# A four-layer graph network on one core: quarter-transposed projections, pre-added row sums, and a scheduler that weighs age against remaining path

One core of one Trainium2 chip (trn2), float32 throughout. The metric is device time of one execution in microseconds (us), lower is better. Engine names: PE is TensorE, PEld its weight loads, DVE is VectorE, ACT is ScalarE, POOL is GpSimd, SP is SyncE (here it only issues DMAs; "SPq" is its queue). A "graph" below is one of the 32 batch elements.

## The reference

`x` is (32, 512, 256), `adj` a (512, 512) 0/1 matrix with about 6% of ones. Each of the four layers is a residual and a normalisation around an attention over the graph:

```
x = LN(x + transformer_block(x, adj))   # 8 heads of 32, FFN; gains are 1, biases 0 in the inputs
x = LN(x + gat(x, adj))                 # layer 1: softmax_m(leaky_relu(s1[n] + s2[m])) @ (x W)
x = LN(x + bilinear_gat(x, adj))        # layer 2: softmax(leaky_relu(x W1 W2^T x^T)) @ (x W3), relu
x = LN(x + gat4(x, adj))                # layer 3: as layer 1 with 4 heads, elu
```

## The kernel before

The kernel is one straight instruction stream per engine. A small planner in Python, run when the kernel is built, decides everything: each operation carries a cost for each engine that may do it, and the planner simulates the engines with these costs, picks the next operation, its engine and its buffers, and emits it. Each engine then executes its instructions in that order; an instruction that waits holds all behind it on that engine. The costs are written in by hand.

```python
# Plan.run: choosing the next operation                        (cut)
tmin = min(c[0] for c in cands)
s, o, e = min((c for c in cands if c[0] <= tmin + 0.05),
              key=lambda c: (not c[1].frees, c[1].graph, -c[1].rank))   # oldest graph first
...
plan = Plan(slots, {...buffer reserves...}, 4, {"DVE": 0.5})            # four graphs open

F = 0.86                                # planner's costs, us: 512 columns on PE
TR = 0.113                              # one PE transpose
TT = {"DVE": cdve(1024)}                # 1024-column tensor_tensor on VectorE
TP = {"POOL": 2.35}                     # 1024-column tensor_tensor on GpSimd

def transposed(xs):                     # 8 PE transposes and 2 evacuations
    ...
            for k in range(KC):
                for j in range(2):
                    nc.tensor.transpose(two(ps)[:, k, j*P:(j+1)*P], T4(xs)[:, 2*s+j, k*P:(k+1)*P], ident)
        op({"PE": 4 * TR}, fn, r=[xs[s]], w=[ps], pre=[xT])
        evac(ps, xT, s, nodes(s), two)

# normalisation, per half of a graph: statistics on DVE, four two-column GpSimd operations, apply on ACT or DVE
op({"DVE": 0.92}, stats, ...)           # bn_stats, bn_aggr
op({"POOL": 1.6}, scales, ...)          # add, pow, negate, multiply
op({"DVE": 0.325, "ACT": cact(C, 2)}, norm, ...)
# checks of value ranges: one to three tiny GpSimd operations
op({"POOL": 0.17 * (1 if lo is None else 3)}, fn, r=[t], ...)

# layer 0: row sums, "packed" is four heads side by side on PE  (cut)
def sums(e, g=g, p=p, ps_s=ps_s):
    for m in (0, 2):
        packed(ps_s, p, m, lambda h: pick[:, g, :], m == 0, m == 2)
op({"PE": 2 * F + 0.13}, sums, r=[p[0][0], p[1][0], p[0][2], p[1][2]], w=[ps_s], pre=[sT])
# layer 0: two wide operations on GpSimd, 128x1024, both inputs in SBUF
op(TP, lambda e: tt(e, T4(xs), T4(xs), be2_sb.t.unsqueeze(1)..., ALU.add), r=[xs, be2_sb], w=[xs])
op(TP, lambda e: tt(e, T4(u), T4(u), g1_sb.t.unsqueeze(1)..., ALU.mult), r=[u, g1_sb], w=[u])

# layers 1 and 3: projection with the score columns
for c in range(NC):
    for i in range(KC):
        nc.tensor.matmul(ps.t[:, :C+e3], T2(xT)[:, i, c*P:(c+1)*P], w.t[:, i, :], start=(i==0), stop=(i==KC-1))

# a graph's start: x in blocks of 32x32, by eight DMAs of 64 KB from the SP queue
op({"SP": 0.8}, block, w=[xZ])
```

## Time and profile before

| | before |
|---|---|
| median of 4 executions | 3234.03 us (3230.48 to 3234.76) |
| profiled span | 3232.5 us |
| PE work, each record at its start-to-start price | 2832 us |
| span less PE work | 400 us |
| PE work / time, 160 to 2960 us ("middle efficiency") | 0.903 |

"Work" is used all through: every PE record is counted at the price that the prediction derives (for instance 0.430 us for a 512-column record), so that the modelled, overlapping ends of matmuls don't blur the sum. The middle efficiency is that work divided by the 2800 us of the window.

### The profile page before, as it was taken

Reading aid. Unit: us, or ns where it says so; the run is one execution under the profiler, and the core shown is the slowest. Engines: PE = TensorE matmul, PEld = TensorE weight load, DVE = VectorE, ACT = ScalarE, POOL = GpSimd, SP = SyncE. Lnnn points to the kernel's source line nnn. Section 1 sums busy time; section 2 is a strip of 40 time slices with the busy share of each in tenths; the row PEclk is TensorE's granted clock in tenths of the full one; section 3 lists DMA queues with packets and bytes.
Section 4 is the critical chain, followed back from the end, with each engine's and each line's share of the span. In section 5 each row is a group of like instructions: output and inputs, shape, how many; then the busy total and the mean of one; then the engine's idle time right before and its main releaser. Section 6 shows DMA issues by size and latency. Waiting matters only on the chain. (4 is left out here: it accounts for less than half of the span.)

```text
span 3232.5 us, 47121 instructions
## 1 busy us (share of the span) xinstructions
PE 3070.4 (95%) x16827; PEld 1892.0 (59%) x16858; DVE 2472.0 (76%) x4819; ACT 1673.5 (52%) x3425; POOL 1278.0 (40%) x2418
## 2 busy tenths in 40 slices
PE   6999999999999999999999999999999999999976
PEld 3656665565656656646656646656646666646543
DVE  6777679777788787797787797777797777797763
ACT  3554555545654555554555554555554555454532
POOL 0434345243444333354233454333354334364330
PEclk8999999999999999999999999999999999999987
DMA  5010110011101110101110111010111010110000
GB/s 123 4 37 14 40 34 24 17 37 34 37 24 37 37 34 21 34 24 37 36 34 20 34 24 37 28 43 10 44 24 37 25 45 4 50 24 24 24 24 21
DMA packets 200338, 101.43 MB, mean 31 GB/s; under 512 B 151585, under 2 KB 186913, under 8 KB 200097
## 3 DMA queue, kind: packets, MB, share of 16 engines
q1 hardware_dynamic: 200096, 98.35, 11.5%
q8 instruction: 135, 2.21, 0.3%
q14 instruction: 107, 0.87, 0.1%
HBM read 81.20 MB, written 17.10 MB: 30 GB/s over the span
## 5 line engine op out<-in xcount | busy, mean ns | idle before, releaser
L332 ACT ACTIVATE b<-ps 128x512 f32<-128x512 f32 x900 | 506.7, 601 | 421.9 <-PE ps L368 153.5
L335 DVE TENSOR_TENSOR b<-b,maskT 128x1024 f32<-128x1024 f32 x512 | 633.7, 1273 | 50.5 <-ACT b L465 50.2
L465 ACT ACTIVATE b<-ps 128x512 f32<-128x512 f32 x1024 | 533.0, 608 | 174.2 <-PE ps L460 174.0
L427 ACT ACTIVATE b<-b,t 128x256 f32<-128x256 f32 x528 | 303.2, 601 | 534.4 <-POOL t L418 473.1
L415 POOL TENSOR_SCALAR t<-t 128x2 f32<-128x2 f32 x384 | 144.6, 376 | 914.5 <-DVE t L410 462.2
L335 DVE TENSOR_TENSOR b<-b,b 128x1024 f32<-128x1024 f32 (+1 forms) x448 | 440.1, 1011 | 35.8 <-ACT b L702 34.4
L416 POOL TENSOR_TENSOR t<-t,mhalf 128x2 f32<-128x2 f32 x384 | 382.7, 997 | 32.0
L720 DVE SCALAR_TENSOR_TENSOR b<-b,s,maskT 128x512 f32<-128x512 f32 x512 | 356.6, 758 | 11.4 <-DMA b<-r 11.4
L460 PE MATMUL ps<-b,b 32*128 32x512 f32 x2048 | 293.2, 640 | 15.3 <-ACT b L332 14.8
L408 DVE BATCH_NORM_STATS2 t<-b 128x6 f32<-128x256 f32 x768 | 285.0, 414 | 3.8
L368 PE MATMUL ps<-b,wqkv_sb 128*128 128x256 f32 x1024 | 250.4, 392 | 13.8 <-DMA wqkv_sb<-in_L_gnn_w_qkv_dram 10.2
L368 PE MATMUL ps<-b,w_sb 128*128 128x256 f32 x1024 | 248.4, 393 | 8.5 <-ACT b L332 8.4
L452 PE MATMUL ps<-b,b 128*32 128x512 f32 x2048 | 251.7, 612 | 1.5 <-DVE b L335 1.2
L728 PE MATMUL ps<-b,b 128*64 128x512 f32 x1024 | 238.7, 606 | 12.1 <-DVE b L720 12.1
L633 PE MATMUL ps<-b,b 128*128 128x257 f32 x1024 | 234.0, 386 | 12.8 <-DVE b L624 12.8
L384 PE MATMUL ps<-w_sb,b 128*128 128x256 f32 x1024 | 244.8, 386 | 0.2 <-ACT b L539 0.2
L666 PE MATMUL ps<-b,b 128*128 128x512 f32 x512 | 240.7, 592 | 1.7
L368 PEld LDWEIGHTS ps<-b,wqkv_sb 128*128 128x128 f32 x1024 | 189.8, 193 | 87.2 <-issue 24.9
L693 PE MATMUL ps<-b,b 128*128 128x257 f32 x1024 | 228.8, 380 | 1.3 <-ACT b L332 1.3
L368 PEld LDWEIGHTS ps<-b,w_sb 128*128 128x128 f32 x1024 | 195.4, 196 | 51.3 <-ACT b L332 17.7
L633 PEld LDWEIGHTS ps<-b,b 128*128 128x128 f32 x1024 | 195.5, 193 | 48.8 <-issue 19.5
L384 PEld LDWEIGHTS ps<-w_sb,b 128*128 128x128 f32 x1024 | 189.0, 190 | 53.1 <-issue 26.1
(124 smaller groups left out, 4291.0 us busy)
## 6 DMA issues: line engine op xcount, KB each, us to landing
b<-r SPq DMA_DIRECT2D x64, 512.0 KB
b<-in_x_dram SPq DMA_DIRECT2D x256, 64.0 KB
b<-in_x_dram SPq DMA_DIRECT2D x32, 512.0 KB
out_dram<-b SPq DMA_DIRECT2D x64, 256.0 KB
b<-r SPq DMA_DIRECT2D x32, 256.0 KB
r<-s SPq DMA_DIRECT2D x128, 0.5 KB
r<-s SPq DMA_DIRECT2D x128, 2.0 KB
b<-in_adj_dram SPq DMA_DIRECT2D x16, 64.0 KB
```

What stands on the lines that cost most here:

```text
L332: nc.scalar.activation(dst, src, AF.Copy)
L335: (nc.vector if e == "DVE" else nc.gpsimd).tensor_tensor(dst, a, b, op)
L368: nc.tensor.matmul(two(ps)[:, k, :], w.t[:, i, col + k * P:col + (k + 1) * P], nodes(s)(xT)[:, i, :], start=(i == 0), stop=(i == KC - 1))
L384: nc.tensor.matmul(two(ps)[:, j, :], T2(xT)[:, i, c * P:(c + 1) * P], w.t[:, i, col:col + C], start=(i == 0 and row is None), stop=(i == K ...
L408: nc.vector.bn_stats(st.t[:, 6 * j:6 * j + 6], T4(y)[:, 2 * s + j, :])
L416: nc.gpsimd.tensor_tensor(mv.t[:, 6:8], mv.t[:, 4:6], mhalf[:, :2], ALU.pow)
L427: nc.scalar.activation(o, i, AF.Identity, bias=b, scale=sc)
L452: nc.tensor.matmul(ps.t[D0 * h:D0 * h + D0, :], lhs(h), T2(p[h // 2][c])[:, h % 2, :], start=start, stop=stop)
L460: nc.tensor.matmul(s[h].t, T2(kT)[r:r + D0, g, c * P:(c + 1) * P], T2(qT)[r:r + D0, g, :], start=True, stop=True)
L465: op({"ACT": cact(512)}, lambda e, c=c, j=j, i=i, s=s, p=p: nc.scalar.activation(T2(p[j][c])[:, i, :], s[2 * j + i].t, AF.Exp, scale=SC0), ...
L633: nc.tensor.matmul(ps.t[:, :C + 1], T2(p[m // 2])[:, m % 2, c * P:(c + 1) * P], hv.t[:, m * (C + 1):(m + 1) * (C + 1)], start=(m == 0), st ...
L720: nc.vector.scalar_tensor_tensor(T2(b)[:, h % 2, :], T2(R[h // 2])[:, h % 2, :], part(1)[:, 0, m, h:h + 1], maskT[m].t, ALU.max, ALU.mult),
```

## The change

Its intent: take 111 us of work from PE, which is busy for 95% of the span, give it to VectorE, and order the graphs so that VectorE's work comes evenly.

```diff
# scheduler: age times 30 less remaining path; five graphs open
-                          key=lambda c: (not c[1].frees, c[1].graph, -c[1].rank))
+                          key=lambda c: (not c[1].frees, c[1].graph * AGE - c[1].rank))
-    plan = Plan(slots, {...}, 4, {"DVE": 0.5})
+    plan = Plan(slots, {...}, 5, {"DVE": 0.5})
-    NB, NS, NT = 42, 12, 24
+    NB, NS, NT = 39, 11, 24
-    TR = 0.113
+    TR = 0.122
# layers 1 and 3: four VectorE transposes of 256 columns, then 32-row quarters on PE
-        xT = transposed(xs)
+            for c in (2 * s, 2 * s + 1):
+                op({"DVE": cdve(256)}, lambda e, c=c: nc.vector.transpose(
+                    xq()[:, c], T4(xs)[:, c, :].rearrange("p (q a) -> p q a", a=32)), r=[xs[s]], w=[xt[s]])
-            for i in range(KC):
-                nc.tensor.matmul(ps.t[:, :C + e3], T2(xT)[:, i, c * P:(c + 1) * P], w.t[:, i, :], ...)
+            for q in range(C // 32):
+                for j in range(4):
+                    r = slice(32 * j, 32 * j + 32)
+                    nc.tensor.matmul(pss[j].t[:, :C + e3], xt.t[r, q * P:(q + 1) * P], w.t[r, q, :], ...)
# layer 0: the sums' chunks added twice over on VectorE, half the sums on PE
+            for j in range(2):
+                op(TT, lambda e, a=p[j][0], b=p[j][2]: tt(e, T2(a), T2(a), T2(b), ALU.add),
+                   r=[p[j][0], p[j][2]], w=[p[j][0]])
-                for m in (0, 2):
-                    packed(ps_s, p, m, lambda h: pick[:, g, :], m == 0, m == 2)
+                packed(ps_s, p, 0, lambda h: pick[:, g, :], True, True)
# projections of layers 0 and 2: one 512-column matmul in place of two of 256 columns
-                    nc.tensor.matmul(two(ps)[:, k, :], w.t[...], nodes(s)(xT)[:, i, :], ...)
+                nc.tensor.matmul(ps.t, w.t[...], T2(xT)[:, i, :], ...)
... (planner's costs of the projections raised by 0.05 to 0.1 us,
...  weights of layers 1 and 3 laid out by quarters through DRAM, node order permuted to match,
...  layer 0's second load of x issued later, 1024-column DVE transpose split in two)
```

## The prediction

> **What bounds the kernel now.** I read the page's busy shares first, then its slices, then windows of the trace, then the timeline of TensorE (PE), and last the chain at the end. The first part says that PE is busy for 95% of the span and VectorE (DVE) for 76%, and the slices show PE full everywhere but in the first slice and the last two:
>
> ```profile
> PE 3070.4 (95%) x16827; PEld 1892.0 (59%) x16858; DVE 2472.0 (76%) x4819; ACT 1673.5 (52%) x3425; POOL 1278.0 (40%) x2418
> ...
> PE   6999999999999999999999999999999999999976
> ```
>
> But matmul ends are modelled and overlap, so busy is not work. The timeline gives the real price: the distance from one start to the next.
>
> ```profile
> 1531.19 1.88 PE L666 MATMUL ps<-b,b 128*128 128x512 f32 x4
> 1532.91 0.38 PE L664 MATMUL ps<-maskN,identb 128*128 128x512 bf16 x1
> ...
> 1542.16 1.91 PE L685 MATMUL ps<-ident,b 128*128 128x128 f32 x16
> 1543.90 7.12 PE L693 MATMUL ps<-b,b 128*128 128x257 f32 x32
> 1550.87 1.04 PE L355 MATMUL ps<-ident,b 128*128 128x128 f32 x8
> 1551.83 1.14 PE L460 MATMUL ps<-b,b 32*128 32x512 f32 x8
> 1552.90 2.02 PE L575 MATMUL ps<-l1w_sb,b 128*128 128x259 f32 x8
> 1554.76 0.60 PE L355 MATMUL ps<-ident,b 128*128 128x128 f32 x4
> ```
>
> Four 512-column records take 1.72 us, so 0.430 each (a float32 matmul leaves two such records); 32 of 257 columns take 6.97 us, so 0.218; 16 transposes take 1.74 us, so 0.109. The eight records of L460, four row groups side by side, take 1.07 us: two passes of 0.430 and 0.21 for going into and out of that tiling. Counting each group's records at these prices: full-width 512 columns 512 x 0.430 = 220; tiled by four (L460, L452, L734) 6144/4 x 0.430 = 660; tiled by two (L728) 1024/2 x 0.430 = 220; 256 or 257 columns 5632 x 0.216 = 1217; L575 1024 x 0.222 = 227; transposes 2304 x 0.109 = 251; bf16 192 x 0.216 = 41. Sum 2836 us of work in a span of 3232. So 396 us are not work. Where they lie, by windows (columns: PE, PEld, DVE, ACT, POOL busy, then PE clock and DMA):
>
> ```profile
> 0.00:80.00 80.00, 49.05 (x252) 25.20 (x253) 54.04 (x125) 28.68 (x58) 4.09 (x57) 0.89 0.54 125
> 160.00:3040.00 2880.00, 2800.07 (x15463) 1733.99 (x15493) 2246.43 (x4345) 1537.45 (x3152) 1188.77 (x2183) 0.99 0.11 30
> 2240.00:2320.00 80.00, 79.95 (x446) 50.00 (x446) 55.48 (x116) 38.23 (x80) 23.56 (x53) 1.00 0.14 37
> 2800.00:2880.00 80.00, 76.83 (x472) 42.66 (x471) 71.57 (x129) 45.64 (x97) 45.25 (x61) 1.00 0.14 37
> 3040.00:3232.00 192.00, 141.28 (x686) 82.63 (x680) 106.50 (x242) 61.10 (x123) 50.45 (x119) 0.86 0.07 22
> ```
>
> Adding the work record by record in these windows gives 33 us in the first 80, 2605 in the 2880 of the middle, 121 in the last 192. Losses: 47 at the start, 275 in the middle, 71 at the end, a few between. In the middle the reader is to see two kinds of stretch: 2240 to 2320 holds 76.2 us of work with DVE at 55, while 2800 to 2880 holds only 70.3 with DVE at 72. DVE's work comes in bunches, and PE loses there. The best stretches still lose 4.7% (tiling changes, weights not loaded ahead), which over 2880 us is 135; the other 140 are waits. At the end, the last graph's L501 starts at 3092.5 and 140 us pass until the kernel ends, with 71 us of PE work left in them; the chain there alternates between engines:
>
> ```profile
> 3188.34 1.65 DMA r<-s
> 3190.07 4.15 DMA b<-r
> 3194.25 6.07 DVE b L720 x9
> 3200.36 5.89 PE ps L728 x12
> ```
>
> **What the Trainium skill says.** "TensorE: Matmul & The Clock Gate", Part 3, says that slices of 32 partitions on distinct row groups run side by side, starts about 4 ns apart, each matmul as long as a full one. The trace agrees, with 7 ns between the starts in L460. "TensorEngine Tiling (Array Packing)", Key Properties: changing the tiling mode drains TensorE. It agrees: the 0.21 us above. "Vector Engine (DVE) Microarchitecture Reference", section 5.2: about 1.04 ns a column and 75 ns an instruction, back to back. Here two 1024-column adds start 1.135 us apart at the median (the skill's figures give 1.14), though each is recorded as 1.25. "VectorE: DVE Perf Modes", The three transpose paths: DVE transposes only within 32x32 blocks, into SBUF. That is why the weights have to be laid out by quarters here.
>
> **The change part by part.**
>
> 1. Layers 1 and 3 lose their PE transposes: 8 a layer, two layers, 32 graphs, 512 of L355's 1024, at 0.109: minus 56 us of PE work. Their 128 evacuations at about 0.60 us leave ACT (minus 77 us busy there, off the path). In their place come 256 DVE transposes of 256 columns. From L435 (1024 columns, 1.163 us start to start) and L602 (32 columns, 0.127) I get 1.044 ns a column, so 0.36 each: plus 92 us of DVE.
>
> 2. The projections of these layers become 32 matmuls of 32 rows in place of 8 of 128 rows. Four run together, so the columns streamed are the same, 227 us. Eight instructions at 7 ns fit into a pass of 0.218. Added: going into and out of the tiling, 64 operations x 0.21 = 13 us. All four results now come at once, into four of the eight PSUM buffers.
>
> 3. Row sums of layer 0: half of the pick records go, 512/4 x 0.430 = minus 55 us of PE; DVE gets 128 more adds of 1024 columns at 1.135: plus 145.
>
> 4. Projections with 512 columns in place of 256: 0.430 against 2 x 0.216, about 2 us. Next to nothing; half as many weight loads, which were hidden already. Two 512-column transposes in place of one of 1024, and the relus halved, are small too.
>
> 5. Scheduler: priority by age times 30 less remaining path, five graphs open in place of four. I compared the order of PE instructions in both compiled programs, with the prices above as a ruler. Work falls from 2834 to 2722 us, which checks parts 1, 3 and 4. In the old order graphs go through in uneven steps (about 115, 70, 70 us of work between their ends, over and over), which is what bunches DVE. In the new one every graph from the fifth to the twenty-ninth is the same 85 us after the one before. At the end, the last graph still has 116 us of work (its own and the graph's before) mixed into the stretch after its layer 0, where it had 71. If that stretch keeps to 140 to 155 us, some 30 to 40 of the 69 lost there come back.
>
> 6. Loading x later, smaller pools, and the extra round trip for the score weights at the start: nothing on the path that I can show, a few us at the start either way.
>
> DVE in all: 2362 us counted start to start, plus 92, 145, 3 for the split transposes and 16 for 48 normalisations that the compiled program moves from ACT to DVE (0.327 each): 2618, or 82 a graph.
>
> Sum: 3232 - 56 - 55 - 2 + 13 = 3132 for work alone. The end gives 30 to 35: 3100. In the middle, the 140 us of waits should shrink with the bunching, but DVE now carries 82 of some 93 us a graph (88%) where it carried 74 of 98. I let these two leave a gain of 35, an estimate with little under it: about **3065 us**, minus 5.2%.
>
> **The rivals.** (a) DVE becomes the bound. For it: in DVE's densest old stretches (such as 2800 to 2880) PE loses about 6 us in 80, and the new load is that dense all the time. At 82 us a graph and 91% use, which is about the most it reaches in an 80 us stretch now, a graph takes 90 us, so the span would be near 3000 if all went well; if DVE order delays PE as in those stretches (88% PE efficiency), 85/0.88 = 97 us a graph and 3150 to 3180, and the change is worth 2 or 3%. Against: the new order spreads DVE's work. (b) The packed projection is issue-bound or serial: 128 instructions in 3.5 us. If row groups overlapped badly (say 1.5 times the time) it costs 0.5 x 227 = 113 us and eats parts 1 and 3 wholly: 3180. Against it: L460's and L734's regular 7 ns. (c) The transposes were hidden anyway. PE waits 123 us ahead of L355 for ACT's normalisation; such a wait would only move to the projection, and the gain of part 1 would shrink towards the bare 56 or under. Since PE is full around it, I count the work as gained. (d) The schedule works as planned: middle at 94% efficiency, 85/0.94 x 32 + about 90 at the ends gives 2985 to 3000.
>
> **Range and chances.** Between (d) and a mild (a): 3000 to 3140 for 8 in 10. Faster by over 2% means below 3170; only (a) or (b) in full miss it: 0.92 faster, 0.07 same, 0.01 slower.
>
> **What would show it.** L606 with 64-record operations about 3.7 us apart and starts 7 ns apart; L365 with 512 records; pick records 512; transposes of 256 columns at a recorded 0.44 us (0.36 apart); DVE busy 2700 to 2780 us and 86% or more of the span; PE work near 2722; windows of the middle alike, with no alternation; the last graph's L520 to the end losing 30 to 45 us rather than 69. I am wrong if L606 takes over 4.5 us an operation, if the DVE transposes cost well over 0.4 us apart, or if the windows show PE waiting for DVE throughout.

## The result, and the profile after

The kernel after takes 3206.04 us (3205.47 to 3209.09, four executions) against 3234.03: ratio 0.9918 [0.99, 0.9935], 0.8% faster, which counts as "same" at 2%. The prediction was 3065 with a range of 3000 to 3140: wrong by 141 us, and outside the range.

Busy times and slices of the kernel after:

```profile
span 3203.9 us, 49645 instructions
...
PE 2994.4 (93%) x17850; PEld 1645.2 (51%) x17882; DVE 2750.8 (86%) x5283; ACT 1553.4 (48%) x3185; POOL 1317.3 (41%) x2417
...
PE   6899999999999999999999999999999999999785
```

The page looks as predicted: PE down, DVE up from 76 to 86%. PE work is 2718 us where 2722 was predicted. But work fell by 114 us and the span by 29, so the time in which PE does nothing useful rose from 400 to 486 us. By place: the first 160 us hold 86 us of work, 20 less than before. Between 160 and 2960 us the efficiency fell from 0.903 to 0.883, which over 2800 us is 56 us more lost. The end loses as much as before: from the last graph's return transposes (L520) to the end 187 us with 116 of work, so 71 lost, against 68 before. Together some 80 of the 86.

The last graph's chain, which in the kernel before could be followed back only over the last tenth of the span, can here be followed over all of it. Shares of the span, by engine:

```profile
DVE 40%; PE 34%; POOL 10%; issue 7%; SPq 3%; ACT 3%; DMA 3%; DVEq 0%; POOLq 0%; ACTq 0%
```

By this chain no single engine bounds the kernel. Most of the path lies outside PE, and GpSimd and the DMA queue, which do little, have 13% of it.

Where does PE wait? Summing PE's idle times by the pair of lines around them gives one place that is new: between the transposes of layer 2 (L717) and its last matmuls (L725) PE loses some 74 us in 33 passages, 28 of them with a wait; the same place before (L685 to L693) lost about 2. The view of L725's own instructions tells it from the other side. EVENT_SEMAPHORE on PEldq is PE's queue standing at a semaphore; the three numbers are ns, least, median and most. First the kernel before, where the line is L693:

```profile
L693 PEldq EVENT_SEMAPHORE  x39: 51/51/51, 164.9 to 3165.5; - x39
```

and the kernel after:

```profile
L725 PEldq EVENT_SEMAPHORE  x37: 51/3022/3026, 196.9 to 3139.9; - x37
its engine sat idle before it (us, times) until:
  POOL t L428: 144.3, 53
```

The waits name L428, the last of the four small GpSimd operations of a normalisation. But L725 reads no normalisation. By my reading of the compiled program, its semaphores are ACT's evacuation of the transposes (L334), DVE's L567 and a memset long done. The trace agrees: all 31 stands of over 1 us end 42 to 44 ns after the end of an L334, also in the first and last graphs, where no L428 ends near. In between, an L428 happens to end within 10 ns of them and is named. The timeline shows how it gets in between (columns: start, us, engine, line, operation, then idle time before and its releaser):

```profile
1051.29 1.89 SPq L1017 DMA_DIRECT2D out_dram<-b  x2
...
1053.22 4.23 SPq L996 DMA_DIRECT2D b<-in_x_dram  x8
...
1058.64 1.43 DVE L447 STREAM_TRANSPOSE b<-b 128x512 f32<-128x512 f32 x2 [0.72 <-DMA b<-in_x_dram]
...
1060.57 0.69 DVE L567 TENSOR_TENSOR b<-ps,b 128x512 f32<-128x512 f32 x1
...
1062.10 1.91 PE L717 MATMUL ps<-ident,b 128*128 128x128 f32 x16
...
1062.36 0.19 POOL L425 TENSOR_SCALAR t<-t 128x2 f32<-128x2 f32 x1 [9.93 <-DVE t L420]
...
1063.80 0.60 ACT L437 ACTIVATE b<-b,t 128x256 f32<-128x256 f32 x1 [2.39 <-POOL t L428]
...
1064.31 3.01 ACT L334 ACTIVATE b<-ps 128x512 f32<-128x512 f32 x6
...
1065.96 8.88 PE L725 MATMUL ps<-b,b 128*128 128x257 f32 x32 [1.95 <-POOL t L428]
```

Read it downwards. The DMA queue issues an output and then the next graph's x, eight issues in 4.2 us; the planner counts 0.8. VectorE's transpose of that x (L447) waits for it and holds L567 and the statistics behind it. So GpSimd's four small operations start late, at 1062.36. ACT's normalisation (L437) waits for them, and ACT's evacuations (L334), which belong to another graph and could have begun at about 1062.6 (after the first four of the sixteen transposes, by their spacing), stand behind L437 in ACT's queue and start at 1064.31. PE waits 1.95 us. In this stretch GpSimd's four are late, not long: they take 1.41 us, less than the 1.6 that the planner counts, and VectorE had stood 0.72 us for x. Over the whole kernel they take 2.06 on average. That this order suits the planner's costs and not the chip's is so far only argued; s4 tests it.

The groups show a second thing. Wide VectorE operations became slower in themselves, and so did the wide GpSimd ones. The line of the shared helper is L335 before and L337 after; L624 became L656. Before:

```profile
L335 DVE TENSOR_TENSOR b<-b,b 128x1024 f32<-128x1024 f32 x256 | 309.6, 1248 | 0.7 <-PE ps L452 0.7
L335 POOL TENSOR_TENSOR b<-b,g_sb 128x1024 f32<-128x1024 f32 x32 | 93.5, 2923 | 142.8 <-ACT b L332 102.3 <-ACT b L539 25.8 <-PE ps L355 13.0
L624 DVE SCALAR_TENSOR_TENSOR b<-b,s,maskT 128x512 f32<-128x512 f32 x128 | 92.1, 779 | 10.4 <-DMA b<-r 10.3
```

After (busy us, then mean ns of one):

```profile
L337 DVE TENSOR_TENSOR b<-b,b 128x1024 f32<-128x1024 f32 x384 | 476.3, 1297 | 0.0
L337 POOL TENSOR_TENSOR b<-b,g_sb 128x1024 f32<-128x1024 f32 x32 | 147.5, 4609 | 77.9 <-DVE b L337 65.4 <-PE ps L365 9.5 <-ACT b L334 3.0
L656 DVE SCALAR_TENSOR_TENSOR b<-b,s,maskT 128x512 f32<-128x512 f32 x128 | 127.7, 1056 | 0.3 <-DMA b<-r 0.3
```

GpSimd's gain multiplication went from 2.9 to 4.6 us, and the 512-column L656 from 0.78 to 1.06. Adding up how much each VectorE instruction took over its group's median (plus 60 ns) gives 52 us before and 101 after. All 62 such instructions after, and all 45 before, overlap a wide GpSimd operation. The Trainium skill has the likely mechanism: "SBUF — State Buffer", Who interferes with whom, says that a VectorE instruction with two SBUF inputs contends with a GpSimd instruction that reads SBUF, not with one that only writes it, and that the loser is blocked for the whole instruction. Two places of the timeline look like that, a pair of VectorE multiplications beside a wide GpSimd operation, and a two-column GpSimd operation beside a VectorE add:

```profile
1037.34 3.05 POOL L337 TENSOR_TENSOR b<-b,g_sb 128x1024 f32<-128x1024 f32 x1 [3.01 <-ACT b L334]
1038.10 4.51 DVE L337 TENSOR_TENSOR b<-b,maskT 128x1024 f32<-128x1024 f32 x2
...
1049.10 1.19 DVE L337 TENSOR_TENSOR b<-b,b 128x1024 f32<-128x1024 f32 x1
1049.38 0.97 POOL L427 TENSOR_SCALAR t<-t 128x2 f32<-128x2 f32 x1
```

The pair took 4.51 us, where two start 1.135 us apart elsewhere and one is recorded as about 1.2; L427 took 0.97 us, where it takes 0.20 at 1051.65. The experiments s3 and s5 test this.

### The profile page after: what moved, and what is told of

It is laid out like the page before. It is cut to its first block, busy times and chain, and to the rows that moved or that the text cites. A ratio compares the mean times of both kernels' runs of the same rounds, so it can differ in the third digit from the quotient of the medians.

```text
span 3203.9 us, 49645 instructions
## 1 busy us (share of the span) xinstructions
PE 2994.4 (93%) x17850; PEld 1645.2 (51%) x17882; DVE 2750.8 (86%) x5283; ACT 1553.4 (48%) x3185; POOL 1317.3 (41%) x2417
## 4 chain that ended last, share of the span: by engine, by line
DVE 40%; PE 34%; POOL 10%; issue 7%; SPq 3%; ACT 3%; DMA 3%; DVEq 0%; POOLq 0%; ACTq 0%
DVE b L337 14%; DVE b L751 8%; PE ps L725 7%; PE ps L606 5%; PE ps L698 5%; PE ps L465 4%; DVE t L418 4%; POOL t L426 4%; DVE b L656 4%; PE ps L473 4%; SPq L996 3%; PE ps L394 2%; PE ps L377 2%; POOL t L425 2%; DMA b<-in_x_dram 2%
## 5 line engine op out<-in xcount | busy, mean ns | idle before, releaser
L337 DVE TENSOR_TENSOR b<-b,b 128x1024 f32<-128x1024 f32 (+1 forms) x576 | 606.5, 1096 | 35.3 <-ACT b L734 33.3
L337 DVE TENSOR_TENSOR b<-b,maskT 128x1024 f32<-128x1024 f32 x512 | 619.8, 1261 | 8.8 <-ACT b L478 8.8
L334 ACT ACTIVATE b<-ps 128x512 f32<-128x512 f32 x772 | 427.7, 604 | 382.2 <-PE ps L365 174.0
L478 ACT ACTIVATE b<-ps 128x512 f32<-128x512 f32 x1024 | 528.3, 609 | 121.2 <-PE ps L473 121.2
L437 ACT ACTIVATE b<-b,t 128x256 f32<-128x256 f32 x480 | 276.7, 602 | 558.8 <-POOL t L428 558.7
L426 POOL TENSOR_TENSOR t<-t,mhalf 128x2 f32<-128x2 f32 x384 | 349.7, 911 | 32.0
L473 PE MATMUL ps<-b,b 32*128 32x512 f32 x2048 | 315.5, 639 | 21.4 <-ACT b L334 21.4
L405 POOL TENSOR_TENSOR acc<-acc,s 128x32 f32<-128x32 f32 (+2 forms) x96 | 58.2, 606 | 610.2 <-DVE s L522 451.9
L725 PE MATMUL ps<-b,b 128*128 128x257 f32 x1024 | 243.1, 397 | 69.5 <-POOL t L428 69.3
L377 PE MATMUL ps<-b,wqkv_sb 128*128 128x512 f32 x512 | 249.4, 613 | 9.8 <-DMA wqkv_sb<-in_L_gnn_w_qkv_dram 9.8
L725 PEld LDWEIGHTS ps<-b,b 128*128 128x128 f32 x1024 | 200.4, 198 | 106.0 <-POOL t L428 75.1
L377 PE MATMUL ps<-b,w_sb 128*128 128x512 f32 x512 | 231.5, 600 | 16.0 <-DVE t L783 15.3
L439 DVE TENSOR_SCALAR b<-b,t 128x256 f32<-128x256 f32 x288 | 119.5, 415 | 146.5 <-POOL t L428 143.8
L665 PEld LDWEIGHTS ps<-b,b 128*128 128x128 f32 x1024 | 194.0, 190 | 47.3 <-issue 18.0
```

The source lines that it names most:

```text
L334: nc.scalar.activation(dst, src, AF.Copy)
L337: (nc.vector if e == "DVE" else nc.gpsimd).tensor_tensor(dst, a, b, op)
L377: nc.tensor.matmul(ps.t, w.t[:, i, col + k * P:col + (k + 1) * P], T2(xT)[:, i, :], start=(i == 0), stop=(i == KC - 1))
L426: nc.gpsimd.tensor_tensor(mv.t[:, 6:8], mv.t[:, 4:6], mhalf[:, :2], ALU.pow)
L473: nc.tensor.matmul(s[h].t, T2(kT)[r:r + D0, g, c * P:(c + 1) * P], T2(qT)[r:r + D0, g, :], start=True, stop=True)
L478: op({"ACT": cact(512)}, lambda e, c=c, j=j, i=i, s=s, p=p: nc.scalar.activation(T2(p[j][c])[:, i, :], s[2 * j + i].t, AF.Exp, scale=SC0), ...
```

## The experiments

Up to three theories are named in the expectations. A: VectorE's load now paces the kernel (the prediction's rival a). B: the order in the engines' queues makes waits; what is added or removed matters less than what stands behind what. C: time follows each engine's share of the chain, some 40% for VectorE. The kernel before took 3231 to 3234 us on the same chips. Correct means agreement with the reference.

### First: the parts one by one

**r1_no_preadd.** The kernel after without the second adds, sums as before; replanned.

```diff
-            for j in range(2):
-                op(TT, lambda e, a=p[j][0], b=p[j][2]: tt(e, T2(a), T2(a), T2(b), ALU.add), ...)
-                packed(ps_s, p, 0, lambda h: pick[:, g, :], True, True)
+                for m in (0, 2):
+                    packed(ps_s, p, m, lambda h: pick[:, g, :], m == 0, m == 2)
```

> The changed kernel without the second additions of the row sums (two chunk sums go to TensorE again): VectorE 145 us less, TensorE 55 us more. Theory A (VectorE's full queue paces each graph: a microsecond of VectorE per graph costs about a microsecond of the 96 us period): the period falls by 3 to 4 us, so 3080 to 3110 us. Theory B (the new order makes queues wait at certain places whatever VectorE carries, above all 2.3 us a graph ahead of layer 2's last matmuls): the added TensorE work shows, 3230 to 3260 us.

Measured: 3173.55 us, 0.9811 [0.9794, 0.9829] of before. So in the kernel after, part 3 costs 33 us where it was to gain 55 less something. The time lies between the forecasts of A and B.

**r2_old_order.** The kernel after with the old priority and four graphs open.

```diff
-                          key=lambda c: (not c[1].frees, c[1].graph * AGE - c[1].rank))
+                          key=lambda c: (not c[1].frees, c[1].graph, -c[1].rank))
-    plan = Plan(slots, {...}, 5, {"DVE": 0.5})
+    plan = Plan(slots, {...}, 4, {"DVE": 0.5})
```

> The changed kernel with the scheduler's old priority (age first) and four open graphs. Theory A: VectorE carries the same, and its work bunches again, 3200 to 3260 us. Theory B: the waits that the new order made go, about 3130 us.

Measured: 3341.77 us, 1.034 [1.0323, 1.0357]. The work of parts 1 to 4 and 6, with less of it on PE, costs 108 us in the old order, more than either theory forecast. Its middle efficiency is 0.848.

**r4_order_only.** The reverse: the kernel before with the new priority and five graphs open.

```diff
# against the kernel before
-                          key=lambda c: (not c[1].frees, c[1].graph, -c[1].rank))
+                          key=lambda c: (not c[1].frees, c[1].graph * 30.0 - c[1].rank))
-    plan = Plan(slots, {...}, 4, {"DVE": 0.5})
+    plan = Plan(slots, {...}, 5, {"DVE": 0.5})
```

> The kernel before with the new priority and five open graphs alone. VectorE carries 74 us a graph, TensorE 88.5. Theory A: VectorE has room, and the even order brings TensorE near the 95% of its best stretches, 3080 to 3130 us. Theory B: the order's waits come with it, no gain, 3220 to 3260 us.

Measured: 3175.57 us, 0.9825 [0.9809, 0.9842]: the order alone gains 57 us, efficiency 0.923. The change as a whole is slower than its scheduler alone: the other parts cost 30 us on top of it.

**r3_no_quarters.** The kernel before with the new order, the pre-adds, the 512-column projections and the later load, but without the quarters of part 1 and 2.

```diff
# against the kernel before: all of the change, but these lines stay as they were
         xT = transposed(xs)            # PE transposes, 128-row projections, natural node order
# ... and so do the 1024-column DVE transpose and the pools (NB, NS = 42, 12)
```

> The changed kernel with layers 1 and 3 (and the node order of layer 0) as before, by TensorE transposes: VectorE some 92 us less, TensorE some 69 us more. Theory A: 2 to 3 us a graph less, 3110 to 3150 us. Theory B: TensorE's work shows, 3250 to 3280 us.

Measured: 3201.78 us, 0.9906 [0.9889, 0.9922]. With the quarters it is 3206.04. The 4 us between them are within the noise: parts 1 and 2 gain nothing here, though they take 43 us of work from PE (56 less 13).

All four times fell outside the ranges of A and of B. What they do show is that the pre-adds, which load VectorE, cost time, and that the order decides how much the rest is worth.

### Second: one cost at a time, with the plan held fixed

In s1 to s3 the planner sees the same operations and costs as in the kernel after, so every queue keeps its order; only what an operation emits differs.

**s1_silent_adds.** The second adds aren't issued; the result is wrong (relative error 0.416).

```diff
-                op(TT, lambda e, a=p[j][0], b=p[j][2]: tt(e, T2(a), T2(a), T2(b), ALU.add),
+                op(TT, lambda e: None,
                    r=[p[j][0], p[j][2]], w=[p[j][0]])
```

> The changed kernel with the same plan and the same order of all other instructions, but the 128 second additions of the row sums are not issued (so the row sums, and the result, are wrong on purpose): VectorE 145 us less, TensorE the same. From the first four runs, two equations (55 us of TensorE against 145 of VectorE gave 33 us, 69 against 92 gave 4) say 0.5 us a microsecond of TensorE and 0.4 of VectorE. Theory A (VectorE's queue alone paces): 100 to 145 us less, 3060 to 3105. Theory C (the pace is a chain that runs through VectorE, TensorE and the waits between them, some 40% of it on VectorE): about 60 less, 3145. Theory B (waits that come from the order, whatever the load): within 20 us of 3206.

Measured: 3172.1 us, 0.9811 [0.9794, 0.9827]. Taking 145 us from VectorE gives 34 us: 0.23 us for each us. A expected at least 100. VectorE's load alone is not what paces this kernel; A falls. C (some 60 us) and B (within 20) missed too, from either side.

**s2_double_sums.** The sums' matmuls twice (relative error 0.239): 55 us more PE work.

```diff
-                packed(ps_s, p, 0, lambda h: pick[:, g, :], True, True)
+                packed(ps_s, p, 0, lambda h: pick[:, g, :], True, False)
+                packed(ps_s, p, 0, lambda h: pick[:, g, :], False, True)
```

> The changed kernel with the same plan, but each row-sum matmul runs twice (twice the sum, wrong on purpose): TensorE 55 us more, all else the same. Theory A: 0 to 15 us more. Theory C: about 27 more, 3233. If TensorE were the bound: 55 or more.

Measured: 3231.6 us, 0.9999 [0.9982, 1.0016]: plus 25 us for 55, or 0.46 for each, which is what C forecast (27). So a us of PE work saved was worth under half a us in this order. Multiplied out for part 3, −55 × 0.46 and +145 × 0.23 make +9; the 33 of r1 has some 24 us of other order in it.

**s3_quiet_pool.** GpSimd's two wide operations aren't issued. The gains are 1 and the biases 0 in these inputs, so the result stays correct.

```diff
-        op(TP, lambda e: tt(e, T4(xs), T4(xs), be2_sb..., ALU.add), r=[xs, be2_sb], w=[xs])
+        op(TP, lambda e: None, r=[xs, be2_sb], w=[xs])
-        op(TP, lambda e: tt(e, T4(u), T4(u), g1_sb..., ALU.mult), r=[u, g1_sb], w=[u])
+        op(TP, lambda e: None, r=[u, g1_sb], w=[u])
```

> The changed kernel with the same plan, but GpSimd's two wide operations a graph (times the first norm's gain, plus the second norm's bias) are not issued; the gain is all ones and the bias all zeros in these inputs, so the result stays right. They read SBUF while VectorE's two-input operations do. VectorE's operations run over their usual length by about 101 us in the changed kernel's trace and 52 in the one before. If that blocking costs on the path: 40 to 100 us less. If not: within 15 us of 3206.

Measured: 3085.38 us, 0.9543 [0.9527, 0.9559], correct: 121 us for 64 operations of an engine that is busy 41% of the time, and more than the 40 to 100 expected. VectorE's time over the usual lengths falls from 101 us to 0:

```profile
L337 DVE TENSOR_TENSOR b<-b,b 128x1024 f32<-128x1024 f32 x384 | 443.5, 1209 | 0.0
```

and PE's loss at layer 2's last matmuls from 74 to 12 us.

**s5_memset_pool.** As s3, but each wide operation is replaced by seven 256-column memsets, which keep GpSimd busy and write SBUF but don't read it. Work buffers are 8 columns narrower to make room.

```diff
+    def fill():
+        for _ in range(7):
+            nc.gpsimd.memset(scr, 0.0)
-        op(TP, lambda e: tt(...), r=[xs, be2_sb], w=[xs])
+        op(TP, lambda e: fill(), r=[xs, be2_sb], w=[xs])
... (the same for the second)
```

> The changed kernel with the same plan, each of GpSimd's two wide operations replaced by seven writes of a constant into a spare tile (about 2.4 us of GpSimd, no read of SBUF; the result stays right, since the gain is one and the bias zero). If the wide operations cost time because they block VectorE's two-input operations: near the run without them, 3085 to 3120 us, and VectorE's overlong durations gone. If they cost time by keeping GpSimd's queue busy ahead of the normalisations: 3170 to 3210.

Measured: 3095.93 us, 0.9572 [0.9556, 0.9588], correct. GpSimd is busy for 1233 us, against 1059 in s3: seven memsets take 2.56 us from first start to last end. Still, 110 of s3's 121 us remain, so GpSimd's busy time is not what costs. The reads are gone, and with them VectorE's time over the usual lengths (0.1 us). But a memset needs no input and nobody reads it: the 129 us for which GpSimd stood idle before its wide operations in the kernel after, waiting for their inputs, are gone too, in s3 as in s5, and no run parts the two. At s1's rate 101 us of VectorE would be worth 23; so either these 101 count more for where they fall, or those waits have a share. VectorE's mean, in this kernel's group (the helper is L342 here):

```profile
L342 DVE TENSOR_TENSOR b<-b,b 128x1024 f32<-128x1024 f32 x384 | 443.8, 1212 | 0.0
```

For VectorE's durations that agrees with the skill's rule on readers and writers, both ways.

**s4_true_costs.** Nothing but three numbers in the planner, set near what the trace of the kernel after shows (for the four of a normalisation 2.06 us on average, 2.26 to the start of the next GpSimd operation where one follows at once; 4.2 for the eight issues); the same instructions, in another order.

```diff
-        op({"POOL": 0.17 * (1 if lo is None else 3)}, fn, r=[t], ...)
+        op({"POOL": 0.5 * (1 if lo is None else 3)}, fn, r=[t], ...)
-            op({"POOL": 1.6}, scales, r=[mv], w=[mv])
+            op({"POOL": 2.3}, scales, r=[mv], w=[mv])
-        op({"SP": 0.8}, block, w=[xZ])
+        op({"SP": 4.3}, block, w=[xZ])
```

> The changed kernel with its planner told what the trace shows for GpSimd and the queue of transfers: 2.3 us in place of 1.6 for the four small operations of a normalisation, 0.5 in place of 0.17 for each check, 4.3 us in place of 0.8 for issuing the eight transfers of a block of x. Same work, another order. Theory B: the waits ahead of layer 2's last matmuls and of VectorE's transposes of x go, 60 to 100 us less. Theories A and C: within 30 us of 3206.

Measured: 3095.53 us, 0.9585 [0.9568, 0.9601], correct: 110 us from three constants. That is theory B, beyond the 60 to 100 that it forecast, and larger than any part of the change. PE's stand at L725 is gone in the median:

```profile
L725 PEldq EVENT_SEMAPHORE  x73: 51/51/1741, 182.7 to 3016.8; - x73
```

and the chain is PE's again:

```profile
PE 75%; DVE 13%; POOL 5%; DMA 2%; SPq 2%; issue 2%; ACT 1%; DVEq 0%; ACTq 0%; POOLq 0%
```

VectorE is still blocked by GpSimd there (79 us over the usual lengths), so s3 and s4 seem to cure different things; e2 and d2 below test it.

### Third: which constants, and for which kernel

**c1_pool_costs** and **c2_sp_cost.** The kernel after with only the two GpSimd constants of s4, and with only the DMA one.

```diff
# c1: "POOL": 0.17 -> 0.5 and 1.6 -> 2.3 alone
# c2
-        op({"SP": 0.8}, block, w=[xZ])
+        op({"SP": 4.3}, block, w=[xZ])
```

> The changed kernel with only the planner's GpSimd costs corrected (2.3 and 0.5 us), the transfer cost left at 0.8. If GpSimd's late normalisations are what the order trips over, most of the 110 us that all corrections gave: 3090 to 3130 us. If the late block of x is: 3170 to 3210.

> The changed kernel with only the planner's cost of issuing a block of x corrected (4.3 us in place of 0.8). The reverse of the run before: 3170 to 3210 us if GpSimd is the cause, 3090 to 3130 if the block of x is.

Measured: 3158.53 us (0.9772 [0.9756, 0.9789]) and 3137.06 us (0.9702 [0.9686, 0.9718]). Minus 48 and minus 69, together 117 against 110 for both at once: near additive, where the expectations had all of it on one side. In c2 PE's loss at L725 falls to 17 us. That does not make the late x the head of that chain, for in c1, which leaves x at 0.8, the loss is 0:

```profile
L725 PEldq EVENT_SEMAPHORE  x65: 51/51/1598, 195.9 to 3085.9; - x65
```

Either correction reorders the queues, and either takes strangers out of this place.

**c3_before_true** and **c4_order_true.** The same three constants in the kernel before, and in the kernel before with the new order (r4).

```diff
# c3, against the kernel before: the three constants of s4
# c4, against the kernel before: the three constants, and
-                          key=lambda c: (not c[1].frees, c[1].graph, -c[1].rank))
+                          key=lambda c: (not c[1].frees, c[1].graph * 30.0 - c[1].rank))
... (and five graphs open)
```

> The kernel before (old work, old priority) with all three corrections. If a blind planner costs every version about the same, 80 to 120 us less, 3110 to 3150 us, and the change's own part would be small. If the old priority was less exposed: 3190 to 3240.

> The kernel before with the new priority and all three corrections: the old work under the best order. If TensorE's 113 us less work pays once the order fits, as the prediction had it, this is 60 to 110 us over the changed kernel with the corrections (3095): 3155 to 3205 us. If the work does not matter: 3080 to 3130.

Measured: 3223.11 us (0.9968 [0.9951, 0.9984]) and 3107.76 us (0.961 [0.9594, 0.9626]). The wrong constants cost 10 us in the old order and 68 in the new one (3175.57 to 3107.76), 110 with the new work. c4's middle efficiency is 0.943, and its chain says that there is nothing left but PE:

```profile
PE 95%; DVE 2%; SPq 1%; issue 1%; DMA 1%; POOL 0%; ACT 0%; DVEq 0%; POOLq 0%; ACTq 0%
```

With right constants the whole of the change's other work is worth only 12 us more (3107.76 to 3095.53), barely clear of the noise: s4's four executions spread over 19 us.

### Fourth: is there a version that beats both?

If s3 and s4 cure different things, both can be had with every operation in place: the constants right, and the two wide operations on VectorE, which takes 1.2 us for one and can't block itself.

**d2_wide_dve.**

```diff
-    TP = {"POOL": 2.35}
+    TP = {"DVE": cdve(1024)}
... (and the three constants of s4)
```

> The changed kernel with the corrected costs and GpSimd's two wide operations moved to VectorE: 73 us more of VectorE work by its own rate, 80 us of overlong durations gone. If blocking is the cost: 3030 to 3080 us. If VectorE's load is: 3110 or more.

Measured: **3030.59 us** (3029.54 to 3031.76), 0.9371 [0.9356, 0.9387], correct: 6.3% faster than before, 5.5% than after. Its busy times, on the page:

```profile
PE 2932.8 (97%) x17882; PEld 1628.8 (54%) x17882; DVE 2672.8 (88%) x5226; ACT 1616.2 (53%) x3306; POOL 1149.5 (38%) x2353
```

VectorE is busy for 78 us less than in the kernel after. It has 64 wide operations more (77 us at 1.2), the replanning moved a net 121 instructions from it to ACT, mostly normalisations (about 50 us at 0.41), and the 101 us of blocking are gone: +77 − 50 − 101 = −74. PE has 83% of the chain, and graphs follow each other every 90.6 us (96.1 after).

**e2_wide_dve_only.** Only the move of the wide operations, with the planner's old constants.

```diff
-    TP = {"POOL": 2.35}
+    TP = {"DVE": cdve(1024)}
```

> The changed kernel with one line changed, the two wide operations on VectorE, and the planner's costs as they were. If the blocking was nearly all of the cost: 3040 to 3090 us. If the planner's blindness counts as much by itself: 3100 to 3150.

Measured: 3139.32 us, 0.9709 [0.9693, 0.9725]. Minus 67 alone; with the constants' 110 that makes 177, and d2 measured 175. The two cures add up. In e2 PE's loss at L725 stays at 61 us while VectorE's blocking is gone, the reverse of s4.

**d1_nopre_true** and **d3_nopre_wide.** The pre-adds asked again: r1 with right constants, and d2 without the second adds.

```diff
# d1: r1's edit and s4's three constants;  d3: d1 and TP = {"DVE": cdve(1024)}
```

> The changed kernel with the corrected costs and without the second additions of the row sums. At the rates of the two runs with an unchanged order (0.23 us a microsecond of VectorE, 0.46 of TensorE) the additions cost 34 and save 25: some 10 us less than with them, 3075 to 3100 us. If the additions pay once the order fits: 3110 to 3150.

> Both of the two before: no second additions, wide operations on VectorE, corrected costs. If both hold, the fastest of all, 3020 to 3070 us; it would beat the kernel before by 5%.

Measured: 3129.1 us (0.968 [0.9664, 0.9696]) and 3062.98 us (0.9476 [0.946, 0.9491]). With right constants the pre-adds gain 34 us (3129 to 3095), with the wide operations moved too they gain 32 (3063 to 3031). In the kernel after they cost 33. Their work is the same in all three. The rates of s1 and s2 had forecast 3075 to 3100 for d1: a rate measured in one order does not carry over to another. Nor is d3 the fastest of all, as was expected.

**e1_old_work_wide.** The last corner: the old work with the new order, right constants, and the wide operations on VectorE.

```diff
# c4, and
-    TP = {"POOL": 2.35}
+    TP = {"DVE": cdve(1024)}
```

> The kernel before (old work: TensorE transposes, full row sums, 256-column projections) with the new priority, the corrected costs and the wide operations on VectorE: the counterpart of the fastest run (3031 us), from which it differs by the work alone. If TensorE's 113 us pay in full: 3130 to 3150 us. If VectorE's added 256 us eat half: 3070 to 3100. If all: 3030 to 3050.

Measured: 3102.18 us, 0.9594 [0.9578, 0.961]. For the old work the move is worth 6 us, which is within the noise. Yet VectorE's time over the usual lengths is 100 us in c4, as in the kernel after, and 0 here. PE paced c4 already (95% of its chain), and unblocking VectorE frees nobody: what blocking costs depends on what waits behind it.

All of it in one table, medians in us. "Work" is parts 1 to 4 and 6:

| order and costs | old work | new work | worth of the new work |
|---|---|---|---|
| old order | 3234 (before) | 3342 (r2) | +108 |
| new order | 3176 (r4) | 3206 (after) | +30 |
| new order, right constants | 3108 (c4) | 3096 (s4) | −12 |
| the same, wide operations on VectorE | 3102 (e1) | 3031 (d2) | −72 |

Without the pre-adds the new work turns about in the same way: +21 us with right constants (d1 against c4), −39 with the wide operations on VectorE too (d3 against e1).

## Why the prediction was wrong

Step by step, as the prediction put it:

**Part 1, the transposes: right.** L365 has 512 records. The 256 DVE transposes are recorded at a median of 0.41 us (0.44 expected) and start 0.34 apart (0.36).

**Part 2, the packed projection: right.** 64-record operations of L606 take 3.72 us from start to next start in layer 1 (259 columns) and 3.83 in layer 3 (268), 3.7 expected, with 7 ns between the starts of a four. Two neighbours in the timeline of PE alone:

```profile
1080.62 3.79 PE L606 MATMUL ps<-l1w_sb,b 32*128 32x259 f32 x64
1084.34 1.92 PE L465 MATMUL ps<-b,b 128*32 128x512 f32 x16
```

Rival (b), a packed projection that is bound by its issue, fell.

**Part 3, row sums: the sizes right.** Pick records are 512. The prediction then took the whole 55 us from the span; s2 shows that a us of PE work was worth 0.46 in this order.

**Part 5, the order: half right.** Graphs do go through evenly, each 95.5 to 98 us after the one before, with PE work 85 in each. (The old order's steps are 67 to 123 us of work in the trace, in a period of five, and not 115, 70, 70; uneven they are.) And the new order does shrink waits by itself (r4, 57 us). But "The end gives 30 to 35" did not come: 71 us are lost there against 68, and with right constants it is still 65 (s4) and 69 (d2).

**DVE's sum: right for the wrong reason.** 2750.8 us busy lies in the 2700 to 2780 expected, but about 100 us of that are VectorE standing blocked beside GpSimd (they vanish in s3); it is not all work.

**The middle: the step that failed.** It was the last term of the sum: "In the middle, the 140 us of waits should shrink with the bunching, but DVE now carries 82 of some 93 us a graph (88%) ... I let these two leave a gain of 35, an estimate with little under it". The middle's losses grew by 56 us. The prediction had counted 13 of these, the changes of tiling, and taken 35 off, so this term missed by 78 us. The end missed by 33 to 38, the start by 20, and some 7 lie between these places: together about 140.

What stood in its place: the prediction compared the order of PE's instructions and asked how evenly work was spread. It didn't ask on which costs the plan rests. In the stretch shown above, the plan puts strangers into one another's queues: a normalisation of one graph ahead of the evacuations of another. That is harmless if the normalisation's inputs come when the planner thinks. They came later: x was issued in 4.2 us where 0.8 was counted, and GpSimd's small operations took longer than counted. Right constants give back 110 us (s4). The second cause lies in GpSimd's two wide operations, beside which VectorE stands blocked: with their reads taken away 110 us come back (s5, with the caveat there), with the operations moved to VectorE 67 (e2). It isn't the added adds that brought the blocking: without them it is 105 us (s1), and the new order alone raises it from 52 to 84 (r4). There, much of it falls on L429, which reads only one wide tile beside scalars from a small one: 0.41 us alone, 2.6 beside a wide GpSimd operation.

**The rivals.** Rival (a) comes near the numbers (88% PE efficiency, 97 us a graph, 3150 to 3180 foretold; 0.883, 96.1 and 3206 measured) but not the mechanism: VectorE's load alone is worth 34 us for 145 (s1), and d2 has, by the sum above, some 25 us more of VectorE work without the blocking and is 175 us faster. A number that fits isn't a cause that's shown. Rival (c), that the transposes were hidden anyway, stays open: parts 1 and 2 gained nothing in this setting (r3), but no run takes them alone with right constants. Rival (d), the middle at 94%, was met by c4 (0.943) and nearly by d2 (0.928), not by the change.

What stays open: why the start lost 20 us and the end gained nothing was not tried alone (with the order alone, r4, the start holds 7 us less work than before and the end loses 53 in place of 68). Nor is it shown why the old order hardly minds the wrong constants (c3, 10 us). And d2 gains 72 of the 114 us of PE work that the change removes; its efficiency is 0.928 against c4's 0.943, so part of the rest is new waiting, perhaps for VectorE at 88%, but no run isolates it.

## What to carry to other kernels

When a plan made from written-in costs decides the order of in-order queues, check these costs against the trace before judging any change that reorders: here three constants were worth 110 us, and the same work was worth +108, +30, −12 and −72 us depending on what surrounded it. A wait names who ended last, not what was waited for; look at the instruction's own semaphores and at what stands ahead in the releaser's queue. And before moving work to VectorE, look for GpSimd operations that read wide SBUF tiles beside it: an engine that is 41% busy can hold up one that is 86% busy. Whether that costs time is another question: 100 us of it cost about 6, within the noise, where PE paced the kernel (c4, e1).

## What the Trainium skill lacked or had wrong

- "SBUF — State Buffer": its rule (a VectorE instruction with two SBUF inputs against a GpSimd one that reads SBUF) held for VectorE's durations in both directions, s3 and s5. It gives no size for a mixed kernel: here 64 GpSimd operations of 1024 columns cost VectorE 101 us beyond its usual lengths, and the kernel 67 (moved to VectorE) to 121 us (not issued).
- "TensorE: Matmul & The Clock Gate": starts on distinct row groups are 7 ns apart here (L606, 64 records), not about 4. Even so four quarters of 32 rows ran as fast as full-height matmuls but for some 0.2 us an operation (3.72 and 3.83 us in the two layers, on average 3.78, against 16 × 0.222 = 3.55).
- "TensorEngine Tiling (Array Packing)": says that changing the mode drains TensorE, without a number; going in and out together cost 0.21 us here.
- "DMA: Bandwidth & Descriptors" lacks, beyond the dispatch, the time for which one issue holds its queue, which is what a planner needs: eight issues of 64 KB on SyncE's queue took 4.2 us, so 0.53 us each, and what stands behind them in that queue starts later.
